# The experts' first layer of 13 blocks as seven half products: one core, fp32

## The chip, the core and the metric

The kernel runs on one core of a Trainium2 chip. A core has a matrix engine (TensorE, PE in the profile; its weight loads are PEld), VectorE (DVE), ScalarE (ACT), GpSimd (POOL) and SyncE (SP), which here mostly issues transfers. They run side by side and wait for each other through semaphores. Each engine takes its own instructions strictly in the order in which the program lists them. PE reads SBUF and writes PSUM, which only DVE and ACT read. The metric is the time of one execution on the chip, in microseconds (us); a version is timed several times and the median counts.

## What is computed

One layer over 4096 tokens of width 256, in fp32: attention with a residual, then a mixture of eight experts with a residual. For every token a gate picks two experts.

```python
x = x + attn(layernorm(x))
h = layernorm(x) @ W_in + b_in
route = top-2 of softmax(h @ W_gate + b_gate), normalised
mid = relu(einsum('nd,edh->neh', h, W1) + b1)      # 256 -> 1024, per expert
eout = einsum('neh,ehd->ned', mid, W2) + b2        # 1024 -> 256, per expert
x = x + einsum('ne,ned->nd', route, eout) @ W_out + b_out
```

The change concerns the line with `W1`.

## The kernel before

Attention comes first, with its scores and the values' sums on PE. It already forms part of its value sums by seven products where eight are usual (`weight_forms`, `value_forms`): sums of the operands are made beforehand on DVE and POOL. While it ends, the tokens are sorted to experts. Each token writes its number into the list of its expert (`put_tile`: a one-column index is cast, then POOL issues an indirect transfer to `slots`), and short tables are worked out on DVE (`plan`).

The experts' part goes through a list `work` of items. Each item is some rows of one or several experts:

- `a` (17) and `b` (7): full blocks of 256 rows of one expert
- `c` (8): 128 rows of one expert
- `d`: twice 64 rows of two experts, `e`: four times 32 rows of four experts, `z`: the late rows

The order is a0 to a8, e0, a9, a10, then d0 a11 c0 a12, d1 a13 c1 a14, d2 a15 c2 a16 c3, d3 b0 c4 b1, d4 b2 c5 b3, d5 b4 c6 b5 c7 b6, and z0. From item 3 on (`steady`) the order of the instructions on PE, DVE and ACT is pinned to the order written; SP's and POOL's are placed by the scheduler.

One turn n of the loop does this: it fetches the slots and rows of item n + 4 (`fetch_rows`: SP loads the slot numbers, POOL issues the gather of h), fetches weights as far as four sets are held (`fetch_weights`, SP, per set two tiles w1 of 512 KB and two tiles w2), computes the first layer of item n + 1 (`hidden`), then the second layer of item n (`contribute`, whose result y is scattered to `parts` by POOL), and turns the rows of item n + 3 so that features lie on partitions (`turn_rows`: 16 transposes on DVE).

The first layer of a full block (`hidden_units`) has eight units. In each, two products of 128x128 weights with 256 columns of turned rows are added up in one PSUM bank, and ACT takes them out with bias and ReLU (L1271). For c, d, e (`hidden_half`) the roles are turned round: the rows are the weights of the product, the expert's w1 is the moving operand in 512 columns, ACT copies the result (L1304), DVE turns it in 16 transposes (L1224) and ACT adds bias and ReLU (L1316).

The second layer of a full block is 16 products of 256 columns, eight for each half of the rows, closed by an addition on DVE (L1341). Every product goes through one helper, so all of PE's lines are L139; the tiles tell them apart: `pm` is a first layer, `pe` a second one, `ps` and `po` belong to attention.

Rings of buffers bind the stages: four sets of weights in the rings `kt` and `v`, 23 buffers of 2 KB per partition in the ring `s` (gathered rows, turned rows, hidden activations), three PSUM banks `mm`, three `o`, two `tr`.

Of the kernel before, what the change touches and what calls it, by code (L numbers as in the profile page):

```python
# [10 lines left out]
F32 = mybir.dt.float32  # L11
I32 = mybir.dt.int32
AF = mybir.ActivationFunctionType
ALU = mybir.AluOpType
# [3 lines left out]
P = 128  # L18
# [5 lines left out]
SB = 256  # L24
# [25 lines left out]
KT = VT = 8  # L50
XB = 4
FORMS = 6
ORDERED = 4
FORMS_FROM = 6

# [2 lines left out]
def preln_attention_moe_kernel(  # L58
# [18 lines left out]
    nc = tc.nc  # L77

    _, S, D = x.shape
    NE, _, FF = W1.shape  # L80
# [3 lines left out]
    ND = D // P  # L84
    NF = FF // P
# [27 lines left out]
    attn = ctx.enter_context(tc.tile_pool(name="attn", bufs=1))  # L113
# [5 lines left out]
    def ps_tr(name):  # L119
        return psum.tile([P, TB], F32, tag="tr", name=name, bufs=2)  # L120

    def ps_o(name):
        return psum.tile([P, TB], F32, tag="o", name=name, bufs=3)
# [14 lines left out]
    def mul(*a, **k):  # L138
        done = nc.tensor.matmul(*a, **k)  # L139
        if ordered:  # L140
            tc.keep_in_program_order(done)
        return done
# [10 lines left out]
    for _ in range(5):  # L153
        done = mul(
            pw[:, :QB],
            lhsT=zeros,
            rhs=zeros.unsqueeze(1).to_broadcast([P, QB // P, P]),
            start=True,
            stop=True,
        )  # L160
# [400 lines left out]
    def piece(name, *shape):  # L561

        return attn.tile([P, *shape], F32, tag="s", name=name, bufs=NS)
# [225 lines left out]
    def value_forms(b):  # L789

        v11, v21 = (vb[b][:, ts(i, KU), :HD] for i in range(KU))
        v12, v22 = (vb[b][:, ts(i, KU), HD + 1 : D + 1] for i in range(KU))
        if b < FORMS - 1:
            tag = ("sq", 4) if b < 4 else ("t23", 1)
            two = attn.tile([P, 2, KU, HD], F32, tag=tag[0], name=f"t23_{b}", bufs=tag[1])
            four = attn.tile([P, KU, HD], F32, tag="t4", name=f"t4_{b}", bufs=FORMS - 1)
        else:
# [22 lines left out]
    def forms_of(g):  # L820
        return min(g // 2, FORMS) if g >= FORMS_FROM else 0

# [68 lines left out]
    def attend_out(r):  # L891
# [15 lines left out]
        for u in range(KU):  # L907
# [12 lines left out]
            ln_stats(1, t)  # L920
        if g % 2 and g // 2 < FORMS and g >= FORMS_FROM:
            value_forms(g // 2)
# [153 lines left out]
    AHEAD = 3  # L1076
    FOUR = AHEAD + 6
    ALONE = FOUR + 2

# [3 lines left out]
    work, blocks_work = blocks_work[:ALONE], blocks_work[ALONE:]  # L1085
# [131 lines left out]
    def pin(done):  # L1217
        if steady:
            tc.keep_in_program_order(done)
# [15 lines left out]
    def hidden(item, got, hT, behind=()):  # L1235


        k, m = item
        _, _, sets, _ = got
        if k in "cdef":  # L1240
            for finish in behind:
                finish()
            return hidden_half(f"{k}{m}", sets, hT)
        units, mid = hidden_units(item, got, hT, behind)
        for do in units:
            do()
        return mid, ()

    def hidden_units(item, got, hT, behind=()):

        k, m = item
        w1, _, c1 = got[2][0]
        mid, behind, by_f = [], list(behind), []

        def unit(f):
            nonlocal behind
            if f % 2 == 0:
                mid.append(piece(f"mid_{k}{m}_{f}", 2, SB))
            pm = ps_mm(f"pm_{k}{m}_{f}")
            for c in range(ND):  # L1260
                pin(
                    mul(
                        pm[:, :SB],
                        lhsT=w1[c][:, ts(f, P)],
                        rhs=hT[:, c, :],
                        start=(c == 0),
                        stop=(c == ND - 1),
                    )
                )
            pin(  # L1270
                nc.scalar.activation(  # L1271
                    mid[f // 2][:, f % 2, :], pm[:, :SB], AF.Relu, bias=c1[:, f : f + 1]
                )
            )
            if f % 2:
                put_one(nc.scalar.copy)
            if f > 2:
                for finish in behind[:2]:
                    finish()
                behind = behind[2:]  # L1280
            by_f.append(mid[f // 2][:, f % 2, :])

        return [partial(unit, f) for f in range(NF)], by_f

    def hidden_half(name, sets, hT):

        rest = P // len(sets)
        raw = attn.tile([P, FF], F32, tag="z1T", name=f"raw_{name}", bufs=1)  # L1290
        for i in range(FF // TB):
            pm = ps_mm(f"pm_{name}_{i}")
            for c in range(ND):
                for j, (w1, _, _) in enumerate(sets):
                    pin(
                        mul(
                            pm[ts(j, rest), :],
                            lhsT=hT[:, c, ts(j, rest)],
                            rhs=w1[c][:, ts(i, TB)],
                            start=(c == 0),  # L1300
                            stop=(c == ND - 1),
                        )
                    )
            pin(nc.scalar.copy(raw[:, ts(i, TB)], pm))  # L1304
        mid = attn.tile([P, NF, P], F32, tag="qT", name=f"mid_{name}", bufs=2)
        squares(mid, raw.rearrange("p (b f) -> p b f", f=P))
        for j, (_, _, c1) in enumerate(sets[1:], 1):
            for f in range(NF):
                on = mid[:, f, ts(j, rest)]
                pin(  # L1310
                    nc.vector.tensor_scalar(on, on, c1[:, f : f + 1], 0.0, ALU.add, ALU.max)
                )

        def finish(f):
            on = mid[:, f, :rest]
            pin(nc.scalar.activation(on, on, AF.Relu, bias=sets[0][2][:, f : f + 1]))  # L1316

        return [mid[:, f, :] for f in range(NF)], [partial(finish, f) for f in range(NF)]

    def contribute(item, got, mid):  # L1320
        k, m = item
        slot, h, sets, c2 = got
        su = h.shape[1]
        rest = P // len(sets)
        y = attn.tile([P, su, D], F32, tag="mx" if su > 1 else "y", name=f"y_{k}{m}", bufs=2)
        for u in range(su):

            name = f"pe_{k}{m}_{u}"
            pe = ps_o(name) if u else ps_tr(name)
            for f in range(NF):  # L1330
                for j, (_, w2, _) in enumerate(sets):
                    pin(
                        mul(
                            pe[ts(j, rest), :D],
                            lhsT=mid[f][:, ts(u, P)][:, ts(j, rest)],
                            rhs=w2[f // (NF // 2)][:, f % (NF // 2), :],
                            start=(f == 0),
                            stop=(f == NF - 1),
                        )
                    )  # L1340
            pin(nc.vector.tensor_tensor(y[:, u, :], pe[:, :D], c2, ALU.add))  # L1341
            put_one()
            put = nc.gpsimd.indirect_dma_start(  # L1343
                out=parts,
                out_offset=bass.IndirectOffsetOnAxis(ap=slot[:, u : u + 1], axis=0),
                in_=y[:, u, :],
                in_offset=None,
                bounds_check=NONE - 1,
                oob_is_err=False,
            )  # L1350

            tc.declare_no_dep(put.ins, group="parts", reason="assignments are distinct")
            tc.add_to_no_dep_group("parts", put.ins)
            if k == "z":
                tc.declare_no_dep(put.ins, group="out", reason="late tokens are others")

# [43 lines left out]
    fill, lgs, got, hTs, z1Ts, rests = [], {}, {}, {}, {}, {}  # L1402
# [54 lines left out]
    first_units, first_turn, first_mid = [], [], None  # L1457
# [24 lines left out]
    for g in range(NT // KU):  # L1482
        b, q = divmod(g, QPB)
        ordered = g >= ORDERED

# [163 lines left out]

    for n in range(1, AHEAD):  # L1650
        hTs[n] = turn_rows(work[n], got[n][1])
    mid, behind = first_mid, ()
    for n, item in enumerate(work):
        steady = n >= AHEAD
        ordered = not steady
# [41 lines left out]
        if n in (AHEAD + 1, len(work) - 1):  # L1697
            for b in range(NB - 1) if n == AHEAD + 1 else (NB - 1,):
                if b < XB:
                    xr = x_block(f"xr{b}")  # L1700
                else:
# [3 lines left out]
                        tag=("z0", "z1", "hr", "qT")[b - XB],  # L1705
                        name=f"xr{b}",
                        bufs=1 if b < NB - 1 else 2,
                    )
                nc.sync.dma_start(out=xr, in_=after[b])
                xrs.append(xr)  # L1710
        following = None
        if n + 2 < len(work):
            following, behind = hidden(work[n + 1], got[n + 1], hTs.pop(n + 1), behind)
        if n == FOUR - 1:
            five, first5, second5 = fetch_weights(work[FOUR + 1], now=False)
# [26 lines left out]
        if n == len(work) - 1:  # L1742
# [1 line left out]
            for b in range(NB - LATE):  # L1744
                collect(b)
            add_up(0)
        contribute(item, got.pop(n), mid)
        if n == 0:
            lg = enter(NB - 1, z1T, attn)
            seen, counting = route(NB - 1, lg, seen, attn, True)  # L1750
# [4 lines left out]
        if n == len(work) - 2:  # L1755
            with tc.If(left_over > 4):
                for item in more:
                    one = fetch_rows(item) + fetch_weights(item, 2 * [("kt", KT)])
                    mid, behind = hidden(item, one, turn_rows(item, one[1]))
# [3 lines left out]
            following, behind = hidden(work[n + 1], got[n + 1], hTs.pop(n + 1))  # L1763
        mid = following
# [5 lines left out]
    for b in range(NB):  # L1770
        following = gather(b + 1) if b + 1 < NB else None
# [34 lines left out]
```

## Time and profile before

| what | us |
| --- | --- |
| three timed runs | 1050.13, 1052.03, 1053.19 |
| median | 1052.03 |
| the profiled execution, whole | 1049.89 |
| its span, first to last instruction | 1048.1 |

The profile is of that one execution. By stage, busy time per engine and the share of the time in which the transfer engines were busy:

| stage, us from the start | PE | DVE | ACT | POOL | DMA share |
| --- | --- | --- | --- | --- | --- |
| 0 to 552.8, attention | 550.39 | 396.75 | 208.11 | 116.75 | 0.28 |
| 552.8 to 599.8, a1 to a3 and the end of the sorting | 47.00 | 34.41 | 12.59 | 25.76 | 0.75 |
| 599.8 to 668.9, a4 to a8 | 69.10 | 30.54 | 18.97 | 22.56 | 0.61 |
| 668.9 to 705.0, e0, a9, a10 | 35.52 | 25.71 | 10.26 | 7.95 | 1.04 |
| 705.0 to 1008.4, the groups with d and c | 301.42 | 239.09 | 96.04 | 81.50 | 0.85 |
| 1008.4 to 1048.1, the weighted sum and the output | 35.49 | 25.12 | 19.27 | 0.98 | 0.71 |

The stages are named by the first layers that PE does in them. A timeline line gives start and length in us from the span's start, engine, line, operation, output<-inputs, shape, and a count; in brackets the idle time before it and what ended that. A release named there is inferred. A product in fp32 is two records on PE. "SPq" is SP's queue: the time is that of the issue, not of the landing.

### The profile page before, as it was taken

The page shows a single profiled execution, that of the slowest core. Times are in us where ns is not written, and L with a number is a line of the kernel's source. Part 1 is how long each engine was busy: PE and PEld are TensorE (multiplying, and loading weights), DVE is VectorE, ACT ScalarE, POOL GpSimd, SP SyncE. Part 2 cuts the span into 40 slices and gives each one's busy share as a digit, 9 for nine tenths or more (in the row PEclk, how much of TensorE's full clock was granted, in tenths as well). Part 3 has the DMA queues.
Part 4 walks back from the last instruction along what each step waited for, and adds up shares of the span by engine and source line. Part 5 has one row for each costly group of instructions (what it writes and reads, how often), then busy time and mean ns, then how long its engine had stood idle before and what let it go on. Part 6 is the DMA issues. An engine that isn't in the chain of part 4 may idle for free. (4 is left out here: it accounts for less than half of the span.)

```text
span 1048.1 us, 17607 instructions
## 1 busy us (share of the span) xinstructions
PE 1038.9 (99%) x5577; PEld 878.5 (84%) x5577; DVE 751.6 (72%) x2421; ACT 365.2 (35%) x823; POOL 255.5 (24%) x311
## 2 busy tenths in 40 slices
PE   9999999999999999999999999999999999999998
PEld 7877889989989989999998888777777767777887
DVE  5766668766957768678787753668887898887645
ACT  2443344434424243324322222132242332242254
POOL 2201332212302121131024632133233232233110
PEclk9999999999999999999999999999999999999999
DMA  7433211121121120105365958699997989987395
GB/s 215 129 78 89 73 41 40 45 63 36 42 48 23 41 56 9 42 3 144 110 196 142 350 146 265 215 367 312 314 339 250 338 258 337 294 285 262 108 335 183
DMA packets 190790, 173.51 MB, mean 166 GB/s; under 512 B 82942, under 2 KB 169922, under 8 KB 190692
## 3 DMA queue, kind: packets, MB, share of 16 engines
q1 hardware_dynamic: 181860, 154.36, 47.6%
q0 software_dynamic: 8288, 17.45, 5.0%
q8 instruction: 46, 0.75, 0.3%
q10 hardware_dynamic: 544, 0.52, 0.1%
q14 instruction: 52, 0.43, 0.1%
HBM read 135.15 MB, written 30.44 MB: 158 GB/s over the span
## 5 line engine op out<-in xcount | busy, mean ns | idle before, releaser
L139 PE MATMUL ps<-qT,zT 128*128 128x256 f32 x1088 | 239.9, 373 | 0.8 <-DVE mx L684 0.8
L139 PEld LDWEIGHTS ps<-qT,zT 128*128 128x128 f32 x1088 | 200.8, 190 | 29.3 <-issue 2.2
L139 PE MATMUL po<-v,s 128*128 128x128 f32 (+1 forms) x672 | 125.8, 320 | 0.0
L139 PE MATMUL pe_a<-w_a,mid_a 128*128 128x256 f32 x544 | 120.8, 380 | 0.0
L139 PEld LDWEIGHTS pe_a<-w_a,mid_a 128*128 128x128 f32 x544 | 102.8, 190 | 18.7 <-issue 4.4
L139 PEld LDWEIGHTS po<-v,s 128*128 128x128 f32 x672 | 107.3, 191 | 9.1
L139 PE MATMUL pm_a<-hT_a,w_a 128*128 128x256 f32 x512 | 113.6, 380 | 0.6 <-DMA w_a<-in_L_ffn_W_dram 0.6
L1271 ACT ACTIVATE mid_a<-pm_a,c_a 128x256 f32<-128x256 f32 x136 | 64.3, 473 | 136.3 <-PE pm_a L139 128.9
L139 PEld LDWEIGHTS pm_a<-hT_a,w_a 128*128 128x128 f32 x512 | 97.0, 190 | 14.5 <-DMA w_a<-in_L_ffn_W_dram 1.0
L678 ACT COPY s<-ps 128x512 f32<-128x512 f32 x120 | 69.4, 581 | 104.6 <-PE ps L139 99.4
L684 DVE TENSOR_TENSOR mx<-ps,mx 128x512 f32<-128x512 f32 x91 | 62.5, 687 | 56.9 <-ACT s L678 56.0
L781 ACT ACTIVATE s<-s 128x512 f32<-128x512 f32 x120 | 73.0, 629 | 72.7 <-DVE s L778 56.0
L467 POOL DMA_INDIRECT slots<-assign,ati x64 | 63.9, 999 | 140.3 <-DVE ati L466 99.6
L778 DVE TENSOR_TENSOR s<-s,pmax 128x512 f32<-128x512 f32 x120 | 77.2, 678 | 9.5 <-PE pmax L145 9.3
L1232 DVE STREAM_TRANSPOSE hT_a<-h_a 32x128 f32<-32x128 f32 x256 | 77.4, 302 | 3.5
L139 PE MATMUL po<-v,sf 128*128 128x129 f32 x384 | 74.5, 276 | 0.1
L1343 POOL DMA_INDIRECT parts<-y_a,slot_a x34 | 34.2, 1006 | 143.2 <-DVE y_a L1341 113.3
L139 PEld LDWEIGHTS po<-v,sf 128*128 128x128 f32 x384 | 58.3, 192 | 0.3 <-DVE sf L817 0.3
L1224 DVE STREAM_TRANSPOSE mid_c<-raw_c 32x256 f32<-32x256 f32 x128 | 55.8, 436 | 1.9
L1136 POOL DMA_INDIRECT h_a<-rows,slot_a x34 | 33.3, 980 | 89.0 <-ACT s L781 36.5
L139 PE MATMUL pm_b<-hT_b,w_b 128*128 128x256 f32 x224 | 49.8, 380 | 1.0 <-ACT mid_b L1271 1.0
L139 PEld LDWEIGHTS pe_b<-w_b,mid_b 128*128 128x128 f32 x224 | 42.3, 190 | 9.5 <-issue 3.6
(350 smaller groups left out, 1637.5 us busy)
## 6 DMA issues: line engine op xcount, KB each, us to landing
w_a<-in_L_ffn_W_dram SPq DMA_DIRECT2D x68, 512.0 KB, 6.3
w_d<-in_L_ffn_W_dram SPq DMA_DIRECT2D x48, 512.0 KB, 8.7
w_c<-in_L_ffn_W_dram SPq DMA_DIRECT2D x32, 512.0 KB, 6.3
w_b<-in_L_ffn_W_dram SPq DMA_DIRECT2D x28, 512.0 KB, 7.5
rows<-hr SPq DMA_DIRECT2D x16, 512.0 KB, 4.9
w_e<-in_L_ffn_W_dram SPq DMA_DIRECT2D x16, 512.0 KB, 6.1
yp<-parts SPq DMA_DIRECT2D x14, 512.0 KB, 11.2
after<-x SPq DMA_DIRECT2D x8, 512.0 KB
```

The costliest lines, as they stand in the source:

```text
L139: done = nc.tensor.matmul(*a, **k)
L467: put = nc.gpsimd.indirect_dma_start(out=slots, out_offset=bass.IndirectOffsetOnAxis(ap=ati, axis=0), in_=assign[:, TOPK * (b * TPB + j) + ...
L678: nc.scalar.copy(flat, ps)
L684: done = nc.vector.tensor_tensor(r.mx, ps, old, ALU.max)
L778: nc.vector.tensor_tensor(s, s, pm[:, :QB].unsqueeze(1).to_broadcast([P, KU, QB]), ALU.subtract)
L781: nc.scalar.activation(s, s, AF.Exp)
L1136: get = nc.gpsimd.indirect_dma_start(out=h[:, u, :], out_offset=None, in_=rows, in_offset=bass.IndirectOffsetOnAxis(ap=slot[:, u : u + 1], ...
L1224: pin(do())
L1232: pin(do())
L1271: nc.scalar.activation(mid[f // 2][:, f % 2, :], pm[:, :SB], AF.Relu, bias=c1[:, f : f + 1])
L1343: put = nc.gpsimd.indirect_dma_start(out=parts, out_offset=bass.IndirectOffsetOnAxis(ap=slot[:, u : u + 1], axis=0), in_=y[:, u, :], in_of ...
```

## The change

**Seven half products.** For an item that `seven_of` picks (a full block from item 4 on, not the two items 9 and 10, whose predecessor in the list is an a, b or c) the first layer is done by Strassen's scheme. Weights and rows are both split in two along the contracted features; the weights are also split into even and odd groups of 128 hidden units, and the rows into two halves of 128. Seven products of 128 columns then take the place of four of 256 per two units, 28 of 128 in place of 16 of 256 per block. 13 blocks are done so: a4 to a8, a10, a12, a14, a16, b1, b3, b5, b6.

**The sums before** (`hidden_forms`, on POOL, written at the end of turn n for item n + 2): four of 512 elements per partition over the weights, three into new tiles and one in place over a part of w1, and four of 128 elements over the turned rows, into one more buffer of the ring `s`.

**The products and the sums after** (`hidden_seven`): four PSUM banks, one per pair of hidden groups. In four steps products go into three regions of each bank; ACT copies out what the later sums need (256 columns after step one, 128 after step two), DVE adds after step three (128 and 256 columns), and ACT applies bias and ReLU, four times from PSUM and eight times on the sums in SBUF. Into this the second layer of the item ahead is woven, product by product (`contribute_units`): one after step two, six after step three, the rest at the end.

**c items** go through `hidden_units` with 128 columns: 16 products of 128 columns in place of 4 of 512; their copies and transposes go. Closing steps of an earlier item now begin at the fifth unit (f > 3) and not the fourth.

```diff
-        if k in "cdef":
+        if k in "def":
+            done = hidden_half(f"{k}{m}", sets, hT)
             for finish in behind:
                 finish()
-            return hidden_half(f"{k}{m}", sets, hT)
+            return done
...
-            if f > 2:
+            if f > 3:
...
+    def seven_of(n):
+        return SEVEN and AHEAD < n < len(work) and work[n][0] in "ab" and n not in ALONG and work[n - 1][0] in "abc"
+
+    def hidden_forms(item, got, hT):
...
+        nc.gpsimd.tensor_tensor(s1, a21, a22, ALU.add)
+        nc.gpsimd.tensor_tensor(s2, s1, a11, ALU.subtract)
+        nc.gpsimd.tensor_tensor(s4, a12, s2, ALU.subtract)
+        nc.gpsimd.tensor_tensor(a21, a11, a21, ALU.subtract)
+        b11, b12, b21, b22 = (hT[:, c, ts(u, P)] for c in range(ND) for u in range(2))
+        t = piece(f"t_{k}{m}", 4, P)
+        nc.gpsimd.tensor_tensor(t[:, 0], b12, b11, ALU.subtract)
+        nc.gpsimd.tensor_tensor(t[:, 1], b22, t[:, 0], ALU.subtract)
+        nc.gpsimd.tensor_tensor(t[:, 2], b22, b12, ALU.subtract)
+        nc.gpsimd.tensor_tensor(t[:, 3], b21, t[:, 1], ALU.subtract)
+        return (
+            (a11, a12, s4, a22, s1, s2, a21),
+            (b11, b21, b22, t[:, 3], t[:, 0], t[:, 1], t[:, 2]),
+        )
+
+    def hidden_seven(item, got, forms, others, later):
...
+        for i in pairs:
+            put(i, 0, xs_, start=True)
+            put(i, 4, ys)
+            put(i, 1, zs, stop=True)
+            pin(nc.scalar.copy(flat[i][:, 2 * P :], banks[i][:, : 2 * P]))
+        for i in pairs:
+            put(i, 5, xs_)
+            put(i, 2, ys, stop=True)
+            pin(nc.scalar.copy(flat[i][:, P : 2 * P], xs_[i]))
+        rest(total - 1)
+        for i in pairs:
+            put(i, 6, xs_)
+            pin(nc.vector.tensor_tensor(flat[i][:, :P], zs[i], flat[i][:, 3 * P :], ALU.add))
+            pin(
+                nc.vector.tensor_tensor(
+                    mids[i][:, :, P:],
+                    banks[i][:, : 2 * P].rearrange("p (u t) -> p u t", t=P),
+                    flat[i][:, P : 3 * P].rearrange("p (u t) -> p u t", t=P),
+                    ALU.add,
+                )
+            )
+        rest(total - 7)
+        for i in pairs:
+            put(i, 3, xs_, stop=True)
+            relu(mids[i][:, 1, :P], xs_[i], 2 * i + 1)
+        finish = []
+        for i in pairs:
+            even, odd = mids[i][:, 0, :], mids[i][:, 1, P:]
+            finish += [partial(relu, even, even, 2 * i), partial(relu, odd, odd, 2 * i + 1)]
+        if not later:
+            for do in finish:
+                do()
+            finish = []
+        rest(0)
...
-        following = None
-        if n + 2 < len(work):
+        following, others = None, None
+        if n + 2 < len(work) and seven_of(n + 1):
+            assert not behind
+            hTs.pop(n + 1)
+            others = contribute_units(item, got.pop(n), mid)
+            following, behind = hidden_seven(
...
-        contribute(item, got.pop(n), mid)
+        if others is None:
+            contribute(item, got.pop(n), mid)
+        if seven_of(n + 2):
+            formed[n + 2] = hidden_forms(work[n + 2], got[n + 2], hTs[n + 2])
```

## The prediction

> **What bounds the kernel now.** I read the page's busy shares first, then PE's timeline, then the queues of the engines that would have to do the new work.
>
> ```profile
> span 1048.1 us, 17607 instructions
> PE 1038.9 (99%) x5577; PEld 878.5 (84%) x5577; DVE 751.6 (72%) x2421; ACT 365.2 (35%) x823; POOL 255.5 (24%) x311
> PEclk9999999999999999999999999999999999999999
> ...
> ```
>
> PE never rests and its clock is full, so PE time removed is time saved, but only while nothing makes PE wait. The price of a product, from PE's timeline, first of a full block and then of the attention's seven products (columns: start, length, engine, line, operation, output<-inputs, shape, count):
>
> ```profile
> 599.82 7.07 PE L139 MATMUL pm_a<-hT_a,w_a 128*128 128x256 f32 x32
> 606.73 7.07 PE L139 MATMUL pe_a<-w_a,mid_a 128*128 128x256 f32 x32
> ...
> 506.94 0.61 PE L139 MATMUL po<-v,s 128*128 128x128 f32 x4
> ...
> 508.51 0.61 PE L139 MATMUL po<-v,s 128*128 128x128 f32 x4
> ```
>
> Start to start, 16 products of 256 columns (two records each) take 606.73 - 599.82 = 6.91 us. Seven products of 128 columns take 508.51 - 506.94 = 1.57 us, 0.224 each, weight loads included. So a half product costs 52% of a whole one.
>
> Now POOL, which is to make the sums, in the stretch where the first changed blocks fall, and the two edges that decide there:
>
> ```profile
> 576.01 1.43 SPq L1183 DMA_DIRECT2D w_a<-in_L_ffn_W_dram  x1
> 579.87 0.98 POOL L467 DMA_INDIRECT slots<-assign,ati  x1 [0.30 <-issue]
> 583.56 0.99 POOL L1343 DMA_INDIRECT parts<-y_a,slot_a  x1 [2.72 <-DVE ati L466]
> 589.24 0.98 POOL L1136 DMA_INDIRECT h_a<-rows,slot_a  x1 [3.41 <-PE pm_a L139]
> 591.79 1.02 POOL L1343 DMA_INDIRECT parts<-y_a,slot_a  x1 [0.31 <-issue]
> 593.12 0.98 POOL L467 DMA_INDIRECT slots<-assign,ati  x1 [0.30 <-issue]
> 606.16 0.97 POOL L467 DMA_INDIRECT slots<-assign,ati  x1 [0.30 <-DVE totale L1016]
> ```
>
> The page's mean of 24% hides that POOL is already back to back from 589 to 607: an indirect DMA every 1.3 us. Its arithmetic, and two rows for later:
>
> ```profile
> 361.80 0.79 POOL L802 TENSOR_TENSOR t<-v 128x256 f32<-128x256 f32 x1
> 560.27 2.35 POOL L1555 TENSOR_TENSOR x<-x,bout 128x1024 f32<-128x1024 f32 x1 [0.18 <-DVE z L344]
> ...
> 685.95 5.04 DVE L1232 STREAM_TRANSPOSE hT_a<-h_a 32x128 f32<-32x128 f32 x16
> 691.05 7.17 PE L139 MATMUL pm_a<-hT_a,w_a 128*128 128x256 f32 x32
> 856.08 1.13 PE L139 MATMUL pm_b<-hT_b,w_b 128*128 128x256 f32 x4 [0.98 <-ACT mid_b L1271]
> 861.67 3.70 PE L139 MATMUL pm_c<-w_c,hT_c 128*128 128x512 f32 x8 [0.86 <-DVE hT_c L1232]
> ```
>
> The transposes of block a10 end (690.99) as PE wants them. The last two lines are stalls, 1.84 us together.
>
> **PE's own work.** The condition (`seven_of`) and the instruction order of the changed program give 13 blocks, not the 14 of the title: a4 to a8, a10, a12, a14, a16, b1, b3, b5, b6. Each goes from 6.91 to 28 x 0.224 = 6.27, saving 0.64: 13 x 0.64 = 8.3 us. The eight c items go from 726.26..729.79 = 3.53 to 16 x 0.224 = 3.58: +0.4 in all. They lose 16 DVE transposes of 0.436 us each (L1224), 7 us per item. Those transposes are what made the two stalls above: DVE stood on mid_c until 843.0 and was late with mid_d and hT_c. Gone: -1.8. Sum -9.7.
>
> **ACT and DVE in a changed block.** DVE adds four times 0.29 (128 columns from PSUM, L697) and 0.42 (256, L1341): 2.8 us, begun some 5 us into the step and wanted by the last four products at 8.4; the transposes before them end at about 5.3. Hidden by seven woven products of the block ahead. ACT: four copies of 0.37 (L635), four of 0.27 (L701), four ACTIVATEs of about 0.33 (between 0.30 and 0.39, L787 and L1316) and eight closing ones of 0.3 to 0.47, some 7 us of a 13 us step. Without the woven products each of these would cost PE its latency. One place has no cover: after b6 PE goes straight to b6's second layer, while ACT has four ACTIVATEs and the first closing one still to do: about +0.9 (0 to 1.5). The four PSUM banks and the extra 's' buffer per block fall free a step or more early; I cost them at nothing. The matmul bound has a bound too: if waits on single products broke the 0.224 rhythm to the 0.28 a lone one takes (L139, 274 to 276 ns), 13 x 28 x 0.05 = 18 us would be lost; the attention's rows say no.
>
> **POOL, the new work.** Per block four sums of 512 elements and four of 128. Rows of that size don't exist; between 0.73 to 0.85 (256) and 2.35 (1024) I take 1.30, plus 0.1 between two, and 0.48 for 128 (bounds: 1.15 and 1.5 for 512). That is 5.6 + 2.3 = 7.9 us per block; with four indirect DMAs 13.1 us in a step of 13.2. In a steady run of full blocks it just fits. It doesn't fit where POOL has a backlog.
>
> *a4 and a5.* The new order puts a4's four weight sums behind the slot scatter of 579.87, waiting for w1 (issued 576.01 to 577.44, landing at the median 6.3 later, about 583). Then come nine indirect DMAs (two scatters of y_a1, two gathers of h_a6, five of slots) with a5's four weight sums among them, and only then a4's first token difference `t[0]`. From 583: 8 x 1.40 + 9 x 1.30 + 0.55 + edges 0.2 = 23.6, so 606.6. PE wants it with its second product of a4, at 599.82 + 0.22 = 600.04. Stall 6.6. Behind the POOL sums stand the last slots, 606 before and some 617 now; for them waits late_slot's load on SP (615.39 before), and behind that the load of a8's w1, wanted 30 us later. The chain goes on: from 583 to a5's `t[0]` stand 11 large sums (15.4), 16 DMAs (20.8) and five small ones (2.9): 622.1. PE, unhindered, is there at 613.2; so both stalls together are 8.9 (bounds 6.5 and 11, from 1.15 and 1.5 per large sum and a landing 5 to 7 later). After that POOL is in front: a6's token sums end near 635, two us ahead of need.
>
> *a10.* `t[0]` heads the group and waits for hT_a10 (690.99); then s1 ends at 693.1, where PE wants both at 691.3: 1.8. Then t1, s2, a21 and s4 end at 697.9, where s4 is wanted at 695.8: 2.1. Together +3.9 (2.5 to 5). Queued behind these sums: the scatter of e0 and the gather of c0, 6 us late, which nobody misses.
>
> *The other seven.* In each, an indirect DMA waiting for y_d or the weights' landing stands before the token sums. Worked as above `t[0]` comes 0.6 to 1.5 us before PE wants it for a12, a14 and b1, level for b3 (+0.3), clear by over 3 for a16, b5, b6. At 1.5 us per large sum three of them slip: 0 to +3.
>
> ```text
> PE -8.3, c +0.4, old stalls -1.8 | a4+a5 +8.9, a10 +3.9, b6 +0.9, b3 +0.3  => +4.3
> ```
>
> The profiled execution took 1049.89 (span 1048.1 and 1.8 around it), so 1054.2. The median of the runs shown, 1052.03, lies 2.1 above it; in their terms 1056.3.
>
> **Two rules.** Until its last product PE never waits longer than 1.1 us in this trace, and every slice shows the full clock. [...] The other: 256 elements cost 0.79 us on POOL (L802), 0.45 on DVE (L815). [...] It speaks against this change; had DVE made the eight large sums before a4's `t[0]` at its own row of 0.68 (L778), the chain would be 5 us shorter.
>
> **Rivals.** (1) The sums hide (not slower): POOL does its sums while descriptors are made for the indirect DMAs, or finishes faster than I think. For: all sums stand one to two steps ahead of use in the order. Against: POOL's records never overlap. It decides once the chain to a4's `t[0]` is under 17 us; the nine DMAs alone take 11.7. With every POOL stall gone: 1049.9 - 9.7 + 0.9 = 1041.1, in the runs' terms 1043. With half of the 12.8 at a4, a5 and a10 left: 1047.5, in the runs' terms 1050. (2) The steady blocks slip too: sums at 1.5 us give +2.1 at a4 and a5, +1 at a10, +3 on the others: 1060.3, or 1062.4. For: margins of about 1 us, DMA busy 85% from 705 on. Against: of POOL's rows only L801, 0.85 per 256, comes near that rate. (3) The change does less than it says: the first layer stays whole in most blocks. Excluded by the order, 13 x 28 half products.
>
> **How the numbers follow.** Forecast (stalls at a4, a5 and a10 outweigh the products saved) 0.55; rival 1 in full 0.11, in part 0.14; rival 2 0.20. The time is the forecast's, 1056. About 0.3% (3.2 us) is what a measurement tells from none: faster means under 1048.9, slower over 1055.2. Rival 1 in full and 0.06 of its part are faster (0.17); the other 0.08 and the forecast's lower end (0.16, its own range being 1051 to 1061) give the same (0.24); the rest is slower (0.59). Reaching to rival 1 in part and to rival 2, the range is 1045 to 1063.
>
> **What would show it.** A PE gap of some 6 us before the second product of a4's first layer, released by POOL; one of 2 at a5; two of 2 at a10; 6.3 us per first layer elsewhere; no stall near 856. The forecast is wrong if POOL's sums of 512 take under 1 us, if PE's gaps are elsewhere, or if half products run slower than 0.224 us.

## The result, and the profile after

The changed kernel takes 1060.95 us (median of 4 runs, 1060.72 to 1062.24) where the kernel before took 1051.5 beside it (1050.13 to 1053.19). The ratio is 1.0095, with a 95% interval of 1.0083 to 1.0107: slower by 9.5 us, where the forecast was 1056. The profiled execution took 1061.0, 11.1 more than that of before.

The head of the page, as the first lines of before were shown:

```profile
span 1059.2 us, 18917 instructions
PE 1038.3 (98%) x6081; PEld 901.4 (85%) x6081; DVE 741.0 (70%) x2397; ACT 397.9 (38%) x963; POOL 342.1 (32%) x415
PEclk9999999999999999999999889999999999999999
```

PE's busy time is what it was, 1038.3 after 1038.9, though 13 blocks need less of it. The clock row says why: two of its 40 slices show an 8 where all had a 9. PE waited there, and then ran slowly. What it waited for, by the view of waits (total us, times, longest):

```profile
PE pm_a L140 <- POOL t_a L1344: 4.8, 1, 4.8
PE pm_a L140 <- POOL t_a L1346: 4.2, 1, 4.2
PE pe_b L140 <- PEq L1880: 1.4, 1, 1.4
PE pm_a L140 <- POOL s_a L1340: 1.1, 1, 1.1
...
PE pm_a L140 <- POOL s_a L1338: 0.9, 1, 0.9
...
PE pm_c L140 <- DVE hT_c L1234: 0.6, 1, 0.6
PE pe_b L140 <- ACT mid_b L1377: 0.5, 1, 0.5
```

PE's timeline at the first three blocks of sevens (blocks done by the seven half products). Each begins with the line "pm_a<-hT_a,w_a" at 599.56 (a4), 628.57 (a5) and 641.73 (a6):

```profile
599.56 0.38 PE L140 MATMUL pm_a<-hT_a,w_a 128*128 128x128 f32 x2
604.76 0.80 PE L140 MATMUL pm_a<-t_a,s_a 128*128 128x128 f32 x2 [4.82 <-POOL t_a L1344]
...
609.61 0.39 PE L140 MATMUL pm_a<-t_a,s_a 128*128 128x128 f32 x2
...
619.71 1.43 PE L140 MATMUL pm_a<-t_a,w_a 128*128 128x128 f32 x4 [4.23 <-POOL t_a L1346]
...
622.74 5.99 PE L140 MATMUL pe_a<-w_a,mid_a 128*128 128x256 f32 x18
628.57 0.38 PE L140 MATMUL pm_a<-hT_a,w_a 128*128 128x128 f32 x2
...
636.95 1.05 PE L140 MATMUL pm_a<-t_a,w_a 128*128 128x128 f32 x8
...
641.73 0.38 PE L140 MATMUL pm_a<-hT_a,w_a 128*128 128x128 f32 x2
```

a5's step (its first layer and the second layer of the block ahead) takes 641.73 - 628.57 = 13.16 us, and so do those of a6 and a7. That is 0.65 less than the 13.81 of two whole layers before. a4's takes 29.01. Its excess of 15.85 us is more than the whole loss. It has two parts. The last four products of the first layer begin 619.71 - 599.56 = 20.15 us into a4's step and 636.95 - 628.57 = 8.38 into a5's: 11.8 us. From there to the end a4 takes 8.86 and a5 4.78: 4.1 us.

The same stretch by windows (length, then busy us and counts of PE, PEld, DVE, ACT and POOL, the granted clock with 1.00 for full, the share of the transfer engines, GB/s):

```profile
599.50:604.80 5.30, 0.48 (x5) 0.27 (x3) 5.17 (x18) 0.00 (x0) 4.80 (x6) 0.81 0.24 78
604.80:609.60 4.80, 4.80 (x22) 4.80 (x23) 4.68 (x34) 1.12 (x3) 4.16 (x6) 0.50 0.20 54
609.60:619.70 10.10, 5.88 (x40) 5.19 (x39) 9.62 (x45) 1.43 (x5) 8.78 (x11) 1.00 0.52 148
619.70:628.50 8.80, 8.51 (x26) 6.70 (x27) 2.15 (x7) 4.23 (x12) 3.97 (x5) 0.61 0.12 37
628.50:641.70 13.20, 13.20 (x90) 12.38 (x89) 8.18 (x26) 6.43 (x20) 9.72 (x11) 1.00 0.41 119
```

Two things are to be seen. After each wait the clock is granted at half: 0.50 from 604.8 to 609.6, where 22 records last 4.80 us that take 2.4 at 0.224 a pair, and a mean of 0.61 from 619.7 on, where the 4.1 us are lost (0.28 of them a short wait for VectorE). And VectorE, the third of the busy times, hardly rests until 619.7: 5.17 of 5.30 us, 4.68 of 4.80, 9.62 of 10.10.

The second wait is put down to a token sum on GpSimd, at 619.18 in its list. That sum belongs to a5, while PE stands before a4's last four products, whose operand `t[3]` was done at 607.24. VectorE's timeline names the real one. In the kernel before, an operation of the planning and the planning's last one:

```profile
596.39 0.21 DVE L991 TENSOR_TENSOR nowb<-nowb,needb 128x8 f32<-128x8 f32 x1
...
608.87 0.17 DVE L1014 CAST base_ie<-basee 128x8 int32<-128x8 f32 x1
```

In the changed kernel, VectorE's timeline over the same work, and a4's first two adds behind it:

```profile
595.30 1.65 DVE L987 TENSOR_TENSOR startb<-uptob,needb 128x8 f32<-128x8 f32 x1
...
597.48 4.36 DVE L992 TENSOR_TENSOR nowb<-nowb,needb 128x8 f32<-128x8 f32 x1
...
614.67 1.62 DVE L1011 TENSOR_SCALAR basee<-basee 128x8 f32<-128x8 f32 x1
...
616.66 0.96 DVE L1012 SCALAR_TENSOR_TENSOR basee<-whosee,basee 128x8 f32<-128x8 f32 x1
...
617.98 0.86 DVE L1015 CAST base_ie<-basee 128x8 int32<-128x8 f32 x1
618.75 0.28 DVE L1396 TENSOR_TENSOR mid_a<-pm_a,mid_a 128x128 f32<-128x128 f32 x1
619.14 0.42 DVE L1398 TENSOR_TENSOR mid_a<-pm_a,mid_a 128x256 f32<-128x256 f32 x1
```

An operation on 8 elements per partition that took 0.21 us takes 4.36. The planning of the experts' tables (`plan`) ends at 618.84 instead of 609.04, and behind it, in VectorE's fixed order, stand a4's eight adds. PE's last four products write into the banks which these adds read; the add that ends at 619.56 is what lets PE go on at 619.71. GpSimd's list at the time of the long operation:

```profile
597.09 0.98 POOL L468 DMA_INDIRECT slots<-assign,ati  x1 [0.17 <-issue]
598.10 1.28 POOL L1339 TENSOR_TENSOR s_a<-s_a,w_a 128x512 f32<-128x512 f32 x1
599.32 1.27 POOL L1341 TENSOR_TENSOR w_a<-w_a 128x512 f32<-128x512 f32 x1
600.54 1.26 POOL L1340 TENSOR_TENSOR s_a<-w_a,s_a 128x512 f32<-128x512 f32 x1
```

The operation on VectorE begins while GpSimd issues an indirect DMA. The three sums of a5's weights end at 601.80, the operation at 601.84. The theory after the result, called "port" below: while GpSimd's sums run, VectorE's small operations stand still, and so the sums delay PE through VectorE as well as through GpSimd's queue. The name is a guess at the cause: no run shows what the two engines share.

### The profile page after: what moved, and what is told of

Same layout as the page of the kernel before. It is cut to its first block, busy times and chain, and to the rows that moved or that the text cites. A ratio compares the mean times of both kernels' runs of the same rounds, so it can differ in the third digit from the quotient of the medians.

```text
span 1059.2 us, 18917 instructions
## 1 busy us (share of the span) xinstructions
PE 1038.3 (98%) x6081; PEld 901.4 (85%) x6081; DVE 741.0 (70%) x2397; ACT 397.9 (38%) x963; POOL 342.1 (32%) x415
## 5 line engine op out<-in xcount | busy, mean ns | idle before, releaser
L140 PE MATMUL pe_a<-w_a,mid_a 128*128 128x256 f32 x544 | 124.7, 385 | 0.0
L140 PE MATMUL pm_a<-hT_a,w_a 128*128 128x256 f32 (+1 forms) x368 | 75.0, 345 | 0.8 <-DMA w_a<-in_L_ffn_W_dram 0.7
L140 PEld LDWEIGHTS pm_a<-hT_a,w_a 128*128 128x128 f32 x368 | 64.2, 196 | 8.1 <-DMA w_a<-in_L_ffn_W_dram 1.1
L140 PE MATMUL pe_b<-w_b,mid_b 128*128 128x256 f32 x224 | 50.1, 381 | 1.9 <-PEq L1880 1.4
L1275 ACT ACTIVATE mid_a<-pm_a,c_a 128x256 f32<-128x256 f32 x64 | 30.3, 473 | 56.1 <-PE pm_a L140 56.1
L1449 DVE TENSOR_TENSOR y_a<-pe_a,c_a 128x256 f32<-128x256 f32 x34 | 14.0, 422 | 52.1 <-PE pe_a L140 52.1
```

The source lines that it names most:

```text
L1275: nc.scalar.activation(mid[f // 2][:, f % 2, :size], pm[:, :size], AF.Relu, bias=c1[:, f : f + 1])
```

## The experiments

Where a ratio is given it is to the kernel before on the same chip, with its 95% interval. On the chip of the first four (e1 to e4) the kernel before took 1059.8 us, and why is open: all four traces have a wait of 3.1 us of PE for VectorE in attention that no other trace has, and it is not the whole difference. So those four are read by their traces first.

**Without a4 (e1).**

```diff
-    ALONG = (FOUR, FOUR + 1)
+    ALONG = (AHEAD + 1, FOUR, FOUR + 1)
```

> a4 alone goes back to the whole first layer; the other twelve blocks keep the seven products. Theory A (the loss sits in a4's step and is made there by GpSimd's sums: the step from 599.56 to 628.57 took 29.0 us where a5's to a8's took 13.2): all of that excess goes, less the 0.65 that a4's products saved, so 1060.95 - 15.85 + 0.65 = about 1046, and faster than before. Theory B (the sums are a load that whichever block comes first has to pay): a5, now the first one, stalls by some 9 us in a4's place, so 1053 to 1056. In the trace, A: no wait of PE over 1 us between 599 and 640; B: one of several us near 614.

Ratio 1.0032 (1.0018 to 1.0047). Theory A fell: the wait went to a5. PE's timeline in e1 has:

```profile
624.64 0.76 PE L140 MATMUL pm_a<-hT_a,w_a 128*128 128x128 f32 x2 [5.52 <-issue]
```

And VectorE's timeline in e1:

```profile
603.30 4.38 DVE L982 CAST neede<-counte 128x8 f32<-128x8 int32 x1
```

But theory B's cause isn't there either. PE waits before a5's very first product, which needs no sum of GpSimd's, only a5's turned rows; VectorE turns them, in the middle of the planning that a5's sums have stretched, and the last of those transposes ends at 624.54. The view names no releaser for this wait.

**The c items alone (e2).** `SEVEN = False`.

> No block uses the seven products; the half blocks (c) keep their new column order. By the prediction's own terms this part is worth +0.4 on PE and -1.8 for the two old stalls near 856 and 862: 1051.5 - 1.4 = 1050.1. Rival: the stall of 0.6 before hT_c at 873.4 in the changed kernel belongs to this part too, then -0.8: 1050.7.

Ratio 1.0007 (0.9995 to 1.002). Neither figure is met. The changed kernel's own trace agrees with nothing gained: a c item takes 744.62 - 740.94 = 3.68 us and not 3.53 (eight times 0.15 lost), the stall of 0.98 is gone, that of 0.86 is still 0.60.

**Filling PE's waits (e3, e8).** Spare products keep PE busy in a4's two waits. `spare(n)` issues n of them, of 128 columns each. In e3 they write into a PSUM bank in which a4's sums are being added up, so a4's part of the output isn't the reference's; in e8 they have their own bank.

```diff
+            if (k, m, i) == ("a", 4, 0):
+                spare(21)
             put(i, 4, ys)
...
         rest(total - 7)
+        if (k, m) == ("a", 4):
+            spare(28)
```

> As the changed kernel, with 21 and 28 spare products of 128 columns (0.224 us each, so 4.7 and 6.3 us) in PE's two waits of block a4, into a part of a PSUM bank that nobody reads. The waits stay, PE is busy in them. Theory clock (PE runs at half clock after a wait of over 4 us: 604.8 to 609.6 at 0.50 and 619.7 to 628.5 at 0.61 of full speed): the first half-clock stretch's 2.4 us are swallowed by the second wait, which ends when VectorE is done, and the second one's 3.2 are saved: about 1057.8, and PEclk at 1.00 throughout. Rival (PE is slow there since GpSimd and VectorE read the same operands): the clock stays at half and the time at 1061.

Ratio 1.0167 (1.0142 to 1.0191). The bank is one that VectorE's adds read, so here the second set stood behind them and came on top of a wait of 7.62 us. Its first half is worth something: with the first wait filled the clock stayed at 1.00 up to the second wait, which grew from 4.2 to 7.6.

> The fill once more, with the 21 and 28 spare products of 128 columns in a PSUM bank of their own, so that the second set doesn't itself stand behind VectorE's adds. Theory clock: the first half-clock stretch (2.4 us lost) only brings PE sooner to the second wait, whose end VectorE sets; the second set covers that wait, no half clock follows it, and its 3.2 us are saved: ratio 1.0065 instead of 1.0095. Rival (the slow products after the waits come from the operands being read by GpSimd and VectorE): granted clock still about 0.5 to 0.6 after the second wait, ratio 1.0095.

Ratio 1.0054 (1.0037 to 1.0071), a little better than expected: 4.2 us less than the changed kernel. PE's timeline in e8, where "idle" is the spare products' bank:

```profile
600.35 0.38 PE L140 MATMUL pm_a<-hT_a,w_a 128*128 128x128 f32 x2
...
613.60 6.41 PE L140 MATMUL idle<-hT_a,w_a 128*128 128x128 f32 x56
619.86 0.61 PE L140 MATMUL pm_a<-t_a,w_a 128*128 128x128 f32 x4
620.86 0.49 PE L140 MATMUL pm_a<-t_a,w_a 128*128 128x128 f32 x2 [0.39 <-DVE mid_a L1406]
...
625.79 0.38 PE L140 MATMUL pm_a<-hT_a,w_a 128*128 128x128 f32 x2
```

Two windows of e8, columns as above:

```profile
612.00:620.00 8.00, 8.00 (x67) 7.79 (x66) 7.40 (x36) 0.00 (x0) 5.84 (x8) 1.00 0.60 184
620.00:629.00 9.00, 8.37 (x56) 7.53 (x55) 4.37 (x14) 5.56 (x16) 7.55 (x9) 1.00 0.41 99
```

The clock is full throughout, the add that frees the first bank ends at 618.99 (619.56 in the changed kernel), and the wait left over is now put down to VectorE by name. So the half clock is the waits' doing. a4's step takes 625.79 - 600.35 = 25.44 us where it took 29.01; 2.9 of these 3.6 us lie behind the second wait (5.93 from 619.86 to 625.79, where it was 8.86), so of the two half-clock stretches it is the second that costs time. The rest of the 4.2 us isn't shown to be the clock's: the 1.4 us at the branch behind b6 (see below) happen to be missing in e8's trace, and a10's waits are 0.5 longer.

**a4's token sums on VectorE (e4, e11).** All four token sums move; that takes the first wait's cause away and leaves the weight sums where they are.

```diff
+        on = nc.vector if (k, m) == ("a", 4) else nc.gpsimd
...
-        nc.gpsimd.tensor_tensor(t[:, 0], b12, b11, ALU.subtract)
+        on.tensor_tensor(t[:, 0], b12, b11, ALU.subtract)
...
```

> As the changed kernel, but a4's four token sums (t0 to t3) are made by VectorE, which has them before its planning work, instead of GpSimd's queue, so the first wait (4.8 us on t0) has no cause left. Theory port (VectorE is the one that decides: its small operations stand still while GpSimd's weight sums run, 4.36 us on one of 8 elements at 597.48, so that a4's adds begin at 618.75): PE only waits later, some 10 us for those adds, and the end hardly moves: 1058 to 1062. Rival queue (the first wait is GpSimd's order and a loss of its own, the second another): 4.8 and the half clock behind it go, 1053.7.

Ratio 1.0169 (1.0145 to 1.0193), too slow for either, on the chip of the first four. The wait is where "port" puts it: 10.71 us before the last four products, released by VectorE. The same edit on another chip:

> a4's token sums on VectorE, a second time, since the first was on the chip on which the kernel before took 1059.8. Theory port: no wait at a4's second product, one of 10 us before its last four, where VectorE's adds come late, half clock after it; ratio 1.0065 to 1.0105, so nothing is gained of the 4.8 us. Rival queue: 1.0025.

Ratio 1.0096 (1.0079 to 1.0113). PE's timeline in e11:

```profile
619.15 2.97 PE L140 MATMUL pm_a<-t_a,w_a 128*128 128x128 f32 x8 [10.91 <-DVE mid_a L1399]
```

The first wait is gone, and nothing clear of noise is gained: PE reaches the adds sooner and waits there till 619.15, 19.46 us into a4's step (begun at 599.69), where it had gone on 20.15 us into it. (The execution that was profiled took 1059.0, the shortest of four up to 1061.91.) GpSimd's queue alone was not the loss.

**Without the blocks that wait (e5, e6, e7),** and the changed kernel beside them.

```diff
-    ALONG = (FOUR, FOUR + 1)
+    ALONG = (AHEAD + 1, AHEAD + 2, FOUR, FOUR + 1)
```

In e6 `FOUR + 2` (a10) is added, in e7 also the condition `n < len(work) - 2` (b6).

> The changed kernel itself once more, beside the next three on their chip, since the kernel before took 1059.8 there instead of 1051.5. If the loss is the same by mechanism, the ratio is again 1.0095. If the lapses that the first four runs showed there (engines idle up to 3 us with nothing that they wait for) hit single products more than whole ones, it is over 1.012.

> a4 and a5 go back to the whole first layer. Theory port: GpSimd's weight sums now come after VectorE has done most of its planning (from 595 to 609 in the kernel before); those of a6 still fall into its end and can put it 5 us back, which just reaches a5's transposes. So no wait of PE over 1 us before a10, and the ratio is 0.996 (11 x -0.64, c +0.4, old stalls -1.2, a10 +2.0, b6 +1.9 = -3.9 of 1051.5). Rival (whichever block is first pays, also behind the planning): a6 stalls by several us, ratio 1.002 or more.

> As the last, and a10 whole too. Its two waits on GpSimd's sums s1 and s4 took 0.89 + 1.14 us: -2.0 + 0.64 against the run without a4 and a5: ratio 0.995. Rival: a10's waits move to a12, ratio unchanged.

> As the last, and b6 whole too: nine blocks of sevens are left, those that a full or half block stands ahead of and no planning or uncovered end touches. b6 cost 0.52 on ScalarE and 1.38 at the branch behind it, and saved 0.64: ratio 0.994, in the time of the first runs 1045. If the branch's 1.38 us is not b6's, it stays in the trace and the ratio is 0.995.

| kernel | blocks of sevens | us | ratio | 95% |
| --- | --- | --- | --- | --- |
| before | 0 | 1050.74 | 1 | |
| changed, again | 13 | 1061.0 | 1.0095 | 1.0078 to 1.0112 |
| e5 | 11 | 1047.01 | 0.9966 | 0.9954 to 0.9977 |
| e6 | 10 | 1045.56 | 0.9953 | 0.9936 to 0.9969 |
| e7 | 9 | 1044.67 | 0.9942 | 0.9926 to 0.9959 |

Each step came out as expected. The intervals of neighbours overlap, so the single steps from e5 to e7 rest on their traces as well, where the waits of a10 and then of b6 are gone. The rival ("whichever block is first pays") fell: a6 as the first doesn't wait. e7 beats both kernels, by 6.1 and 16.3 us. The head of its page:

```profile
span 1042.4 us, 18583 instructions
PE 1033.8 (99%) x5985; PEld 896.0 (86%) x5985; DVE 723.8 (69%) x2365; ACT 387.1 (37%) x915; POOL 315.4 (30%) x383
PEclk9999999999999999999999999999999999999999
```

**The sums with nobody waiting for them (e9).** e7, with a4's and a5's weight sums put back into GpSimd's queue; a4 and a5 are computed whole and don't use them, and the fourth sum goes into a spare tile, not over w1.

```diff
...
+        nc.gpsimd.tensor_tensor(s1, a21, a22, ALU.add)
+        nc.gpsimd.tensor_tensor(s2, s1, a11, ALU.subtract)
+        nc.gpsimd.tensor_tensor(s4, a12, s2, ALU.subtract)
+        nc.gpsimd.tensor_tensor(s1, a11, a21, ALU.subtract)
...
+        if n + 2 in (AHEAD + 1, AHEAD + 2):
+            load(work[n + 2], got[n + 2])
```

> The best version so far (nine blocks of sevens, ratio 0.9942), with a4's and a5's four weight sums of 512 elements put back into GpSimd's queue at their old place; nobody uses what they make, and no product waits for GpSimd there. Theory port: VectorE's operations of 8 to 56 elements again stand still for 1 to 4 us while those sums run (595 to 602), its planning ends 5 to 8 us later, a5's transposes with it, and PE waits 3 to 6 us before a5's first layer, near 613, at half clock for a moment after it: ratio 0.998 to 1.002. Rival (only the waits for the sums' results cost anything): ratio 0.994 as without them, no small operation of VectorE over 1 us there.

Ratio 1.0005 (0.9995 to 1.0015): eight sums that feed nothing cost 0.63% or some 6.6 us (ratio 1.0005 against e7's 0.9942; the two ran on different chips). Two lines of VectorE's timeline in e9:

```profile
599.82 1.22 DVE L994 TENSOR_TENSOR nowb<-nowb,nowa 128x8 f32<-128x8 f32 x1
601.04 1.29 DVE L1007 TENSOR_TENSOR gridb<-gridb,startb 128x56 f32<-128x56 f32 x1
```

GpSimd's timeline in e9 at the same time:

```profile
599.74 1.28 POOL L1366 TENSOR_TENSOR s_a<-w_a,s_a 128x512 f32<-128x512 f32 x1
600.98 1.27 POOL L1367 TENSOR_TENSOR s_a<-w_a 128x512 f32<-128x512 f32 x1
```

And PE's timeline in e9 at a5's first layer:

```profile
618.44 9.71 PE L140 MATMUL pm_a<-hT_a,w_a 128*128 128x256 f32 x32 [4.57 <-issue]
```

From 599.7 on VectorE gets through to its next long operation once per sum, and each lasts as long as the sum: 601.04 and 602.33 on the one side, 601.02 and 602.25 on the other. PE, which needs no sum here, waits 4.57 us for a5's turned rows and then takes 9.71 for a layer of 7.07, at a granted clock of 0.50 at first. In VectorE's list there is no wait from 593.1 until those rows are turned (618.34), so it is the stretched operations that make them late. This is the run that settles "port", in the sense given above: that the sums hold VectorE, whatever the two engines share.

**Memsets in place of the sums (e10).** As e9, with one sum of one element and six memsets per block instead of the four sums; four memsets of each block fall into this stretch.

> As the last, but in the place of each block's sums GpSimd does one sum of one element and memsets of the same 512-element tiles, which write SBUF and read nothing. If what blocks VectorE is the reading side of a port (Theory port, reading), its TENSOR_TENSORs with two inputs in SBUF are no longer stretched and the ratio is near 0.994 to 0.996; if the writing side or any GpSimd work does it, operations of VectorE are stretched as long as the memsets last, and the time lies nearer to that of the sums.

Ratio 0.9956 (0.994 to 0.9973), which overlaps e7's. Four memsets are 1.9 us of GpSimd where four sums are 5.0, and they still stretch VectorE. GpSimd's timeline in e10:

```profile
596.44 1.47 POOL L1366 MEMSET s_a<- 128x512 f32 x3
```

VectorE's timeline in e10:

```profile
595.82 2.11 DVE L979 TENSOR_SCALAR counte<-counte 128x8 int32<-128x8 int32 x1
```

The one that stood still here is an operation with one tensor input, until the memsets end (597.91, 597.93); it began 0.6 us before them, beside the issue of an indirect DMA. The operations with two inputs stood behind it in VectorE's order, and none met the memsets alone. So the run shows that GpSimd work which reads nothing can hold VectorE too, and doesn't settle what reading and writing do in it.

## Why the prediction was right in sign and wrong in size

By its own steps, in the scale of the profiled runs (forecast +4.3, measured +11.1):

| step | forecast | measured |
| --- | --- | --- |
| PE's products, 13 blocks | -8.3 | -8.4 (13.16 a step for 13.81) |
| c items | +0.4 | +1.2 (3.68 for 3.53, eight times) |
| two old stalls | -1.8 | -1.2 (one of 0.60 stays) |
| a4 and a5 | +8.9 | +15.85, all at a4 |
| a10 | +3.9 | +2.7 (a step of 15.92 for 13.2) |
| b6 | +0.9 | +0.5, and 1.4 at the branch behind it |
| b3 | +0.3 | none |

What is left to 11.1 is small: 0.5 before a9, 0.3 less ahead of a4, 0.6 less at the end; half a microsecond has no place.

*The half products* were right: 0.224 us each, 0.65 saved per block, and nine blocks of it are e7's gain.

*GpSimd's queue at a4* was right in mechanism and too long. `t[0]` began at 604.24 and not about 606; the sums of 512 elements took 1.24 from start to start where 1.40 was taken, those of 128 took 0.41. PE stood 4.82 us where 6.6 was forecast. But it is hardly a loss of its own: without it (e11) the last four products began 19.46 us into the step in place of 20.15.

*The failing step* is the one headed "ACT and DVE in a changed block", with its word "Hidden". It counted VectorE's adds by their lengths and gave them a steady block's start, "some 5 us into the step". At a4 they stand behind the planning's hundred small operations, and what GpSimd's sums do to these was put at nothing: the prediction doesn't name them. The sums put their end 9.8 us back (609.04 to 618.84). That sets where a4's last four products begin, and with it 11.8 of the 15.85 us; the wait of 4.82 lies inside them, the second wait of 4.23 ends them. The forecast had a wait of 2.3 at a5 on GpSimd in its place. Both of its bounds for a4 and a5 (6.5 and 11) lie below the 15.85, because neither had VectorE in it.

The sign was in the trace of before. Operations of 8 to 128 elements fill the stretch where GpSimd would get its sums, and some of them already last until the issue of an indirect DMA on GpSimd ends. In the kernel before, on VectorE and on GpSimd:

```profile
605.40 0.45 DVE L990 TENSOR_SCALAR nowe<-nowe 128x8 f32<-128x8 f32 x1
604.86 0.99 POOL L1343 DMA_INDIRECT parts<-y_a,slot_a  x1 [0.45 <-DVE ati L466]
```

Both end at 605.85; the same line's operation in the table before took 0.16 (599.43).

The rows of the changed kernel show who stands still beside whom. Beside GpSimd's sums a TENSOR_TENSOR took 4.36 us, a TENSOR_SCALAR 1.62, a SCALAR_TENSOR_TENSOR 0.96 and a CAST 0.86, where the same operations of the kernel before took 0.21, 0.17, 0.17 and 0.17; each of the four ended within 0.04 us of a sum's end (601.80, 616.25, 617.59, 618.81). The 4.36 us spans the end of an indirect DMA's issue (597.09 to 598.07) and three sums in a row. Other operations went on: a4's adds, with one input in PSUM, kept their 0.28 us (620.20) beside GpSimd's sum of 620.00 to 621.27, and the transposes of turned rows took 0.30 and 0.31 (616.32, 617.64) beside two sums and have the same mean of 302 ns in both kernels. That fits the steady blocks, where VectorE does only these (in a5's step 16 transposes and 10 additions with an input in PSUM) and the sums hide.

*The clock* has no term in the sum. The 2.4 us that the half clock took after the first wait cost little, since the wait behind took most of them up: of the 3.6 us by which e8 shortened a4's step, with both waits filled, 0.7 lie ahead of the last four products, and in e3, with the first wait filled, the second grew from 4.23 to 7.62. But the second wait brought a second half-clock stretch, and no wait stood behind that one to take it up: it is the other 4.1 of a4's 15.85 us, of which e8 won back 2.9. That is the second thing that the sum lacks.

*a10* was right in place, 0.89 and 1.14 us on `s1` and `s4`, and too high by 1.2: PE came to a10 0.53 us after its transposes had ended (703.83, 703.30) and not level with them (691.05, 690.99), and the sums were shorter than taken.

*b6.* The 0.52 on ScalarE was foreseen. The 1.4 us at the branch (L1880) was not. It shows in 5 of 9 profiles with b6 as sevens (1.1 to 1.4 us; 0.3 in a sixth) and in none of 5 without. e7 gained 0.9 by leaving b6 whole; what makes the branch late stays open.

*The rivals.* The sums don't hide, and the steady blocks don't slip. The waits forecast at a4's second product and twice at a10 are there, the one at a5 is not; that GpSimd's work could slow VectorE was in none of the cases. The 1060.95 lies close to rival 2's 1062.4, but that is chance: its mechanism, sums of 1.5 us and steady blocks that slip, isn't there. Against rival 1 it was said that GpSimd's records never overlap; in the trace of before its short arithmetic does, by up to 0.08 us, an indirect DMA never.

## What to carry to other kernels

Work given to GpSimd can be paid for on VectorE too (some 6.6 us in e9, where nothing used the sums): before moving sums there, list what VectorE does in that stretch, however small, and which of it is of the kinds that stood still here (operations on two tensors in SBUF, TENSOR_SCALARs, CASTs; 4.36 us for 0.21). Follow the delay through VectorE's fixed order to the first thing PE needs (here adds, and in two experiments transposes), because the wait's named releaser can be a bystander. A scheme that pays in steady state is best begun where its sums meet no such stretch: leaving out 4 of 13 blocks turned 9.5 us of loss into 6.1 of gain.

## What the runs showed of the hardware that was not expected

Back-to-back sums on GpSimd can hold VectorE off longer than one of them: 4.36 us in the changed kernel, where in e9 VectorE got one long operation through per sum (1.22 and 1.29 us). The issue of an indirect DMA on GpSimd can hold VectorE as well, by less: 0.45 us for an operation of 0.16 in the kernel before.

The half clock outlasted the waits, and not by the same time. Windows inside the slow stretches of the changed kernel show 0.50 (603.5 to 609.6, 622.0 to 625.5), those between and after them 1.00. Taking the clock for one or the other throughout (an estimate), it was at half for 2w(1 - m) of a window of w us with a mean of m. So it lasted 6.8 us around the end of the first wait of 4.82 us (by the windows, 2.0 of the wait and 4.8 behind it), 6.9 after the second of 4.23 (8.80 us at a mean of 0.61) and 6.9 in e9 around the end of a wait of 4.57 (6.5 at 0.75, 5.0 at 0.64); in e11, with a wait of 10.91, it lasted 10.2 (12.5 at 0.77, 4.5 at 0.51), 4.4 of it from 619.0 on. So the price of a wait is not one fixed figure here; what sets it no run shows.
